# The tail of a four-layer graph network on one core: the last two row pairs, instead of one, taken tile by tile with plain products

## Chip, core and metric

The kernel runs on one NeuronCore of a Trainium2 chip. The time is device microseconds of that core for one launch; lower is better. Engine names are those of the profile: PE is TensorE's matmul, PEld its weight load, DVE is VectorE, ACT is ScalarE, POOL is GpSimd, SP is SyncE, which here issues the DMAs.

## What is computed

Input x has 128 graphs of 64 nodes with 512 features (8192 rows), in float32; adj is one 64 x 64 graph for all of them. Four layers follow each other, each as x = layernorm(x + layer(x)).

```python
# layer 0: sum of messages
deg[:, None] * (x @ Wi.T + b) + adj @ (x @ Wj.T)
# layer 1: four attention heads, an output layer with attention, a feed-forward part
h   = elu(gat(x, adj, W_heads, a_heads))     # 4 heads, 512 -> 512 each
out = elu(gat(h, adj, W_out, a_out))         # 2048 -> 512
y   = relu(out @ w1 + b1) @ w2 + b2 + out
l1  = (y - mean) / sqrt(var + 1e-5) * gamma + beta
# layers 2 and 3: one attention head each
attn = softmax(where(adj, leaky(e_src[i] + e_dst[j], 0.2), -inf))
l2  = attn @ (x @ W)
```

gat is the same kind of attention with a leak of 0.01. The score vectors e_src and e_dst are dot products of rows of x with W @ a.

## The kernel before

**Tiles and pairs.** A tile is 128 rows (two graphs). T = 2 tiles make a pair of 256 rows, and there are NP = 32 pairs, numbered 0 to 31. Aggregation over the neighbours is done first (A x), then the product with the weights. Most products are Strassen-Winograd products of a 2 x 2 split: `strassen` (L685) and `seven` (L633) take seven products of half size instead of eight. For a pair the split is by tile, by halves of the inner dimension and by halves of the 512 output columns, so that each product is a chain of matmuls with 256 columns into the PSUM tiles stx and sty. The seven weight factors (11, 12, 21, 22 and the sums T1 to T4) are computed once on POOL (`stage_stream`, L580), stored in DRAM, and streamed in for every pair by `part_from` (L613): the 512-row weights into a ring called "ws" with NWS = 4 places, the 256-row ones (w2, W2, W3) into "wk" with 6. The sums on the data side are POOL's too (`sums`, L709).

**Stages of a pair.** `stage_first` (L887) is layer 0; `stage_scores` (L937) the heads' scores (f), the attention and the aggregated rows ys; `stage_heads` (L1007) the four heads (PSUM tiles stx_h, sty_h, results hT); `stage_project` (L1044) the product with W_out (stx_o, sty_o, result who) and the dots for the output attention (f_1o). `stage_out` (L1084) is the output attention (`out_attention`, L1068: transposes bc_1o and pt_1o, attention rows e_1o and aT_1o), the aggregation op, elu, the transposes oTp, w1 (hidp), w2 (stx_y, sty_y), and the norms. `stage_gat` (L1138) is layer 2 or 3: dots with the rows r (f), `attention` (L819: bc, e, pt), the copy to aT, the aggregation gp, and the product with W2 or W3 (stx, sty). `stage_late` (L1289) runs `stage_out` and both `stage_gat`.

**The last pair.** Pair 31 ends otherwise. `stage_last` (L1192) loads w2, W2 and W3 as they are (raw, named w2_last, W2_last, W3_last), b2 and gamma (rows_last), does the output attention of the pair and loads the score rows of both layers. `stage_tile` (L1209) then takes each of the two tiles by itself from the aggregation op on: w1 for 128 rows, and w2, W2 and W3 as plain products, `plain` (L1216), four matmuls of 512 columns into yp and z. Its attention is that of one tile (64 columns instead of 128), and `norms` (L855) and `normalize` (L737) are as for the others. `moments` (L726) puts the two steps of 1/sqrt(var) on POOL (rs).

**What sets the order.** The program text doesn't: every call is recorded as a step (`Plan.note`, L188). The stages are generators that a queue of due times advances (`start`, L1303, and the loop behind it, in units of TURN = 107); a step's number in this recording is its rank. `Plan.play` (L327) adds to the rank the value of LATER (L48) for the step's engine and tile name, with S or E for the first 11% and the last 7% of all steps. `Plan.order` (L229) is a list scheduler: with a cost for each call and a hand-over time (WAIT, L41), it gives each engine the ready step of the lowest rank, and gives out the places of the pools. The order that comes out is what is emitted; on the chip each engine takes its steps in that order. All instructions have the line of the call in `play`, 336, so this text tells them apart by tile names.

**The lines around the change**, from the loop that starts the stages (L1314):

```python
at, pace, rest = {NP - 2: (2.0, 0.8, 0.0), NP - 1: (1.3, 0.6, 0.0)}.get(
    p, (1.42, 1.0, 5.0)
)
if p < NP - 1:
    start(TURN * (p + at), 10 * p, stage_late(p, pace, rest))
else:
    start(TURN * (p + at), 10 * p, stage_last(p))
    for t in range(T):
        start(TURN * (p + at), 10 * p + 1 + t, stage_tile(p, t))
```

Of the kernel before, what the change touches and what calls it, by code (L numbers as in the profile page):

```python
# [12 lines left out]
FP = mybir.dt.float32  # L13
# [7 lines left out]
P = 128  # L21
EPS = 1e-5
NEVER = -3.0e38
T = 2
TURN = 107.0
# [2 lines left out]
NA = 2  # L28
NWS = 4
NWK = 6  # L30
UNITS = 3
AHEAD = 4

# [4 lines left out]

WAIT = 0.152  # L41
NEAR = 150
SLACK = {"tensor": 0.8, "sync": 0.4}

# [1 line left out]


LATER = {  # L48
    "gp:never/S": -100, "gp:rs_i": -60, "gp:s_o/S": -20, "gp:ys/E": -40, "sc:aT": -100,
    "sc:aTg/S": 20, "sc:elu/S": -40, "sc:hT": 120, "sc:oT": 60, "sc:who": -80, "sc:xT": -200,  # L50
    "sc:xT/S": -180, "sc:ys/S": 132, "sy:beta/S": -12, "sy:raw_w": 180, "te:fp/S": -20,
    "te:hidp/E": -40, "te:hidp/S": 28, "te:l": 29, "te:l/S": 69, "te:pt": -28, "te:pt/E": 200,
    "ve:e": -29, "ve:e/S": 40, "ve:f_o/S": -120, "ve:hT": 100, "ve:has": 200, "ve:mv": -100,
    "ve:mv/E": 100, "ve:mx": -20, "ve:o": -140, "ve:r": -40, "ve:r/E": 40, "ve:sh": 10,
    "ve:sm": -80, "ve:st": -13,
}


# [315 lines left out]
def gnn_stack_kernel(  # L374
# [24 lines left out]
    nc = Plan(tc)  # L399
    NT, D = x.shape  # L400
    N = adj.shape[0]
    H = W_heads.shape[0]
# [30 lines left out]
    def rows(srcs, name, tag="rows"):  # L433

        bufs = {"rows": 2, "A": NA}.get(tag, 1)
        t = unit.tile([P, 2, D], FP, tag=tag, bufs=bufs, name=f"rows_{name}")
        for i, src in enumerate(srcs):
            nc.sync.dma_start(out=t[:, i, :], in_=src.partition_broadcast(P))
        return t
# [66 lines left out]
    score = {}  # L506
# [561 lines left out]
    def out_attention(p):  # L1068

        while p not in outs:  # L1070
            yield 1.0
        who, f = outs.pop(p)
        pt = yield from attention(
            f, 0.01, mask1, fill1.to_broadcast([P, N]), None, f"1o_{p}"
        )
        aT = unit.tile([P, T, N], FP, tag="aT", bufs=2, name=f"aT_1o_{p}")
        with nc.soon():
            for b in range(2):
                for t in range(T):
                    nc.scalar.copy(aT[ts(b, N), t, :], pt[ts(t, N), ts(b, N)])  # L1080
        yield 2.0
        return who, aT
# [106 lines left out]

    shared = {}  # L1190

    def stage_last(p):  # L1192

        raw = {}
        for name, src, tag, bufs in (("w2", w2, "ax", 1), ("W2", W2, "ys", 2), ("W3", W3, "ys", 2)):
            raw[name] = unit.tile([P, KC, D], FP, tag=tag, bufs=bufs, name=f"{name}_last")
            nc.sync.dma_start(out=raw[name], in_=src.rearrange("(c p) o -> p c o", p=P))
        r = unit.tile([P, 2, D], FP, tag="hT", bufs=H, name="rows_last")
        for i, src in enumerate((b2, gamma)):
            nc.sync.dma_start(out=r[:, i, :], in_=src.partition_broadcast(P))  # L1200
        who, aT = yield from out_attention(p)
        o = xp.tile([P, T, D], FP, tag="x", name=f"o_{p}")
        shared.update(raw=raw, rows=r, who=who, aT=aT, o=o)
        yield 2.0
        for name in ("2", "3"):
            shared[name] = rows([score[name][s, :] for s in range(2)], f"{name}_{p}")
            yield 2.0

    def stage_tile(p, t):  # L1209

        while "3" not in shared:
            yield 1.0
        x, o, r, raw = xs[p][:, t, :], shared["o"][:, t, :], shared["rows"], shared["raw"]
        who, aT = shared["who"], shared["aT"]

        def plain(lhsT, w, into, name):  # L1216
            ps = psum.tile([P, D], FP, tag="b", name=name)
            for k in range(KC):
                nc.tensor.matmul(
                    ps, lhsT=lhsT(k), rhs=w[:, k, :], start=(k == 0), stop=(k == KC - 1)  # L1220
                )
            nc.vector.tensor_tensor(into, ps, into, ALU.add)

        ps = psum.tile([P, D], FP, tag="b", name=f"op_{p}_{t}")
        with nc.together():
            for b in range(2):
                nc.tensor.matmul(
                    ps[ts(b, N), :], lhsT=aT[ts(t, N), b, :], rhs=who[ts(t, N), b, :],
                    start=True, stop=True,
                )  # L1230
        elu(o, ps)
        yield 3.0
        both = unit.tile([P, 2, KC, P], FP, tag="A", bufs=NA, name=f"oT_{p}_{t}")
        oT, hid = both[:, 0, :, :], both[:, 1, :, :]
        ps = psum.tile([P, KC, P], FP, tag="b", name=f"oTp_{p}_{t}")
        with nc.together():
            for k in range(KC):
                nc.tensor.transpose(ps[:, k, :], o[:, ts(k, P)], ident)
        nc.scalar.copy(oT, ps)
        nc.gpsimd.tensor_tensor(o, o, r[:, 0, :], ALU.add)  # L1240
        yield 3.0
        ps = psum.tile([P, KC, P], FP, tag="b", name=f"hidp_{p}_{t}")
        for c in range(KC):
            with nc.together():
                for k in range(KC):
                    nc.tensor.matmul(
                        ps[:, c, :], lhsT=w1_sb[:, k, ts(c, P)], rhs=oT[:, k, :],
                        start=(k == 0), stop=(k == KC - 1),
                    )
        for c in range(KC):  # L1250
            nc.scalar.activation(
                hid[:, c, :], ps[:, c, :], AF.Relu, bias=b1_sb[:, c : c + 1]
            )
        yield 4.0
        plain(lambda k: hid[:, k, :], raw["w2"], o, f"yp_{p}_{t}")
        norms(o, x, r[:, 1, :], f"{p}_{t}")
        yield 8.0
        for name in ("2", "3"):
            f = small.tile([P, 2], FP, tag="f1", name=f"f_{name}_{p}_{t}")
            for s in range(2):  # L1260
                junk = unit.tile([P, D], BF, tag="junk", name=f"j_{name}_{p}_{t}_{s}")
                nc.vector.tensor_tensor_reduce(
                    junk, x, shared[name][:, s, :], 1.0, 0.0, ALU.mult, ALU.add,
                    accum_out=f[:, s : s + 1],
                )
            yield 2.0
            pt = yield from attention(
                f.unsqueeze(2), 0.2, mask2, never.to_broadcast([P, N]), has, f"{name}_{p}_{t}", 1
            )
            aT = unit.tile([P, P], FP, tag="s3", bufs=2, name=f"aT_{name}_{p}_{t}")  # L1270
            nc.gpsimd.memset(aT, 0.0)
            for b in range(2):
                nc.scalar.copy(aT[ts(b, N), ts(b, N)], pt[:, ts(b, N)])
            yield 2.0
            gT = unit.tile([P, KC, P], FP, tag="s2", bufs=2, name=f"gT{name}_{p}_{t}")
            ps = psum.tile([P, KC, P], FP, tag="b", name=f"gp{name}_{p}_{t}")
            with nc.together():
                for c in range(KC):
                    nc.tensor.matmul(
                        ps[:, c, :], lhsT=x[:, ts(c, P)], rhs=aT, start=True, stop=True  # L1280
                    )
            nc.scalar.copy(gT, ps)
            yield 3.0
            plain(lambda k: gT[:, k, :], raw[f"W{name}"], x, f"z{name}_{p}_{t}")
            normalize(x, f"{name}_{p}_{t}")
            yield 6.0
        nc.sync.dma_start(out=out[ts(p * T + t, P), :], in_=x)

    def stage_late(p, pace, rest):  # L1289

        for later in stage_out(p):
            yield later * pace
        for name in ("2", "3"):
            yield rest
            for later in stage_gat(p, name):
                yield later * pace
# [6 lines left out]
    def start(at, order, stage):  # L1303
        heapq.heappush(queue, (at, order, stage))

    for p in range(NP):
        if p < AHEAD:
            start(TURN * (0.2 * p - 1.2), 10 * p + 4, stage_first(p))
        else:
            start(TURN * (p - 1.1), 10 * p + 4, stage_first(p))  # L1310
        start(TURN * (p - 0.5), 10 * p + 3, stage_scores(p))
        start(TURN * (p + 0.6), 10 * p + 2, stage_project(p))

        at, pace, rest = {NP - 2: (2.0, 0.8, 0.0), NP - 1: (1.3, 0.6, 0.0)}.get(  # L1314
            p, (1.42, 1.0, 5.0)
        )
        if p < NP - 1:
            start(TURN * (p + at), 10 * p, stage_late(p, pace, rest))
        else:
            start(TURN * (p + at), 10 * p, stage_last(p))  # L1320
            for t in range(T):
                start(TURN * (p + at), 10 * p + 1 + t, stage_tile(p, t))
    start(0.0, 10 * NP, stage_heads())
    start(-1.15 * TURN, 0, score_weights(
        [head_rows(w) for w in w_h], a_h, "h", lambda h: head_sums(w_h[h])
# [67 lines left out]
```

## Time and profile before

| | |
|---|---|
| median of 3 runs | 3310.98 us (3309.94 to 3311.04) |
| the profiled execution | 3313.95 us, span 3312.2 us |
| PE busy | 3265.2 us, 21268 matmul records |
| PE weight load busy | 2881.8 us |
| DVE, ACT, POOL busy | 2374.4, 1364.6, 1724.0 us |
| DMA | 726.08 MB, mean 219 GB/s |
| granted PE clock | 0.994 |

The span reaches from the first to the last instruction of the core. A float32 matmul appears as two records. In a row of a group, the name left of the arrow is the tile written, then the tiles read, then the shape. A wait row reads "who waited <- for whom: total, times, longest". Names have lost their numbers: stx_o is the PSUM tile of any pair's W_out product, z that of any plain product with W2 or W3. PE's matmuls are pipelined, so that the length of a record is more than the distance to the next one; distances between starts are used here where a price is needed.

### The profile page before, as it was taken

The numbers are of one execution on the slowest core, as the hardware profiler recorded it, in microseconds if no ns is written. First come the engines' busy times: TensorE is split into PE (matmuls) and PEld (weight loads), VectorE is DVE, ScalarE is ACT, GpSimd is POOL, SyncE is SP. The second block draws the span as 40 slices with busy tenths as digits, with TensorE's granted clock in tenths as the row PEclk, the third lists the DMA queues.
The fourth block names the chain that finished last, engine by engine and source line by source line (L and its number), as shares of the span: only waits on it lengthen the run. The fifth ranks groups of instructions, "written<-read, shape, count | busy, mean of one in ns | idle before, by whom it ended". The sixth has DMA issues, their size and how long they took to land.

```text
span 3312.2 us, 60000 instructions
## 1 busy us (share of the span) xinstructions
PE 3265.2 (99%) x21268; PEld 2881.8 (87%) x21268; DVE 2374.4 (72%) x5668; ACT 1364.6 (41%) x3226; POOL 1724.0 (52%) x1860
## 2 busy tenths in 40 slices
PE   8999999999999999999999999999999999999997
PEld 4888888898988989989889988888889899898885
DVE  5467767777777777777777777777777767777766
ACT  2434344343444434444443443434444344343442
POOL 6745445554555555455454555645554455554442
PEclk9999999999999999999999999999999999999998
DMA  8956666767667676667766667676666766667652
GB/s 303 338 177 215 221 203 215 234 208 237 211 210 233 213 247 197 200 230 221 242 204 220 212 217 236 214 226 208 214 233 208 246 201 202 229 216 238 227 183 77
DMA packets 306584, 726.08 MB, mean 219 GB/s; under 512 B 34240, under 2 KB 43504, under 8 KB 306288
## 3 DMA queue, kind: packets, MB, share of 16 engines
q1 hardware_dynamic: 306288, 722.26, 67.1%
q8 instruction: 171, 2.80, 0.3%
q14 instruction: 125, 1.02, 0.1%
HBM read 688.69 MB, written 33.44 MB: 218 GB/s over the span
## 4 chain that ended last, share of the span: by engine, by line
PE 91%; DVE 4%; DMA 3%; POOL 1%; issue 1%; ACT 0%; SPq 0%; POOLq 0%; DVEq 0%; ACTq 0%
PE stx_h L336 13%; PE stx_o L336 13%; PE stx L336 12%; PE sty_h L336 10%; PE sty_o L336 9%; PE sty L336 9%; PE hidp L336 7%; PE yp L336 4%; PE gp L336 3%; PE stx_y L336 3%; PE sty_y L336 2%; PE axp L336 2%; PE l L336 1%; PE op L336 1%; PE oTp L336 1%; DMA d_f<-f 1%
## 5 line engine op out<-in xcount | busy, mean ns | idle before, releaser
L336 DVE CUSTOM_DVE_ANT_0 j<-x,rows 128x512 bf16<-128x512 f32 x736 | 584.1, 794 | 94.3 <-DMA rows<-d_h 75.6
L336 PE MATMUL stx_h<-ys,wh 128*128 128x128 f32 x3072 | 403.8, 275 | 0.7 <-DVE hT L336 0.7
L336 PEld LDWEIGHTS stx_h<-ys,wh 128*128 128x128 f32 x3072 | 381.1, 192 | 22.3 <-DVE sh L336 5.7
L336 POOL TENSOR_SCALAR rs<-mv 128x1 f32<-128x1 f32 x256 | 104.1, 407 | 406.2 <-DVE mv L336 392.2
L336 ACT COPY hT<-stx_h 128x256 f32<-128x256 f32 x384 | 143.0, 372 | 384.6 <-PE stx_h L336 378.6
L336 ACT ACTIVATE x<-x,sh,rs 128x512 f32<-128x512 f32 x256 | 207.2, 813 | 223.6 <-DVE sh L336 221.0
L336 PE MATMUL sty_h<-ys,wh 128*128 128x128 f32 x2048 | 273.8, 277 | 0.0
L336 PEld LDWEIGHTS sty_h<-ys,wh 128*128 128x128 f32 x2048 | 254.4, 192 | 9.0 <-issue 0.5
L336 PE MATMUL stx_o<-ws_wo_T,s_o 128*128 128x256 f32 x1024 | 246.0, 383 | 0.5 <-ACT who L336 0.5
L336 DVE TENSOR_TENSOR x<-stx,x 128x256 f32<-128x256 f32 x360 | 150.8, 420 | 132.1 <-PE stx L336 131.0
L336 PE MATMUL sty_o<-ws_wo,hT 128*128 128x256 f32 x1024 | 243.2, 380 | 0.1
L336 PE MATMUL hidp<-oT,w 128*128 128x256 f32 (+1 forms) x1056 | 228.9, 373 | 0.0
L336 PEld LDWEIGHTS hidp<-oT,w 128*128 128x128 f32 x1056 | 194.0, 190 | 24.9 <-ACT oT L336 0.2
L336 PEld LDWEIGHTS stx_o<-ws_wo_T,s_o 128*128 128x128 f32 x1024 | 190.2, 191 | 28.4 <-ACT who L336 2.1
L336 PEld LDWEIGHTS sty_o<-ws_wo,hT 128*128 128x128 f32 x1024 | 190.8, 191 | 25.6 <-issue 1.1
L336 DVE SCALAR_TENSOR_TENSOR hT<-elu,hT 128x512 f32<-128x512 f32 x256 | 174.9, 684 | 43.3 <-ACT elu L336 41.3
L336 POOL TENSOR_TENSOR ys<-ys,t 128x256 f32<-128x256 f32 x128 | 102.9, 814 | 189.8 <-PE sty_h L336 189.4
L336 ACT ACTIVATE elu<-hT 128x512 f32<-128x512 f32 x256 | 153.0, 599 | 108.7 <-DVE hT L336 104.6
L336 POOL TENSOR_TENSOR rs<-rs,mhalf 128x1 f32<-128x1 f32 x256 | 173.4, 677 | 21.1
L336 DVE BATCH_NORM_STATS2 st<-x 128x6 f32<-128x512 f32 x256 | 176.5, 689 | 5.1
L336 DVE TENSOR_TENSOR hT<-sty_h,hT 128x256 f32<-128x256 f32 x256 | 107.2, 420 | 81.2 <-PE sty_h L336 69.3
L336 ACT COPY ys<-yp 128x512 f32<-128x512 f32 x256 | 132.2, 602 | 78.4 <-PE yp L336 71.7
(205 smaller groups left out, 7629.3 us busy)
## 6 DMA issues: line engine op xcount, KB each, us to landing
ws_wo_T<-d_wo_T SPq DMA_DIRECT2D x256, 512.0 KB, 3.9
ws_wo<-d_wo SPq DMA_DIRECT2D x192, 512.0 KB, 5.3
ws_W_T<-d_W_T SPq DMA_DIRECT2D x248, 256.0 KB, 4.2
rows<-d_h SPq DMA_DIRECT2D x240, 256.0 KB, 4.7
ws_w_T<-d_w_T SPq DMA_DIRECT2D x112, 512.0 KB, 4.9
ws_W<-d_W SPq DMA_DIRECT2D x186, 256.0 KB, 4.1
ws_w<-d_w SPq DMA_DIRECT2D x84, 512.0 KB, 5.2
rows<-d SPq DMA_DIRECT2D x128, 256.0 KB, 4.3
```

What stands on the lines that cost most here:

```text
L336: getattr(getattr(self.tc.nc, s.engine), name)(*map(real, args), **{k: real(v) for k, v in kw.items()})
```

## The change

Pair 30 now ends as pair 31 did: its output attention is done for the pair, and from the aggregation op on each of its tiles runs through `stage_tile`, with hidp for 128 rows at a time and plain products with w2, W2 and W3. `stage_last` is split. What all four tiles share (the raw weights, b2, gamma, and the score rows) is loaded by `stage_last()` once; the score rows of layer 2 now stand in a place of the "hT" pool and those of layer 3 in one of the "ws" ring. `stage_out_last(p)` does the output attention of one pair; o of pair 30 is in the "o" pool, that of pair 31 in the "x" pool as before. LAST holds the due times of these stages. WAIT goes from 0.152 to 0.153, and the LATER values are another list (36 entries before, 50 now).

```diff
+LAST = (2.0, 1.3, 1.0)
...
-WAIT = 0.152
+WAIT = 0.153
...
 LATER = {
-    "gp:never/S": -100, "gp:rs_i": -60, "gp:s_o/S": -20, "gp:ys/E": -40, "sc:aT": -100,
...
+    "gp:bones": -160, "gp:fill": -140, "gp:hT/S": -20, "gp:never/S": -100, "gp:o": 200,
+    "gp:raw_W": 40, "gp:raw_W/S": -80, "gp:raw_wo/S": -100, "gp:rs/E": 180, "gp:rs_i": -400,
...
+    "sc:who": -80, "sc:xT/S": -320, "sy:d_w_T/S": 26, "sy:degb": 31, "sy:degb/S": 13,
+    "sy:raw_wo": 40, "sy:ws_wo_T": -280, "te:fp/S": -20, "te:hidp/S": 28, "te:l": 20,
...
-    def stage_last(p):
+    def stage_last():
...
-        who, aT = yield from out_attention(p)
-        o = xp.tile([P, T, D], FP, tag="x", name=f"o_{p}")
-        shared.update(raw=raw, rows=r, who=who, aT=aT, o=o)
+        shared.update(raw=raw, rows=r)
         yield 2.0
         for name in ("2", "3"):
-            shared[name] = rows([score[name][s, :] for s in range(2)], f"{name}_{p}")
+            tag, bufs = {"2": ("hT", H), "3": ("ws", NWS)}[name]
+            shared[name] = unit.tile([P, 2, D], FP, tag=tag, bufs=bufs, name=f"rows_{name}_last")
+            for s in range(2):
+                nc.sync.dma_start(
+                    out=shared[name][:, s, :], in_=score[name][s, :].partition_broadcast(P)
+                )
             yield 2.0
 
+    def stage_out_last(p):
+
+        who, aT = yield from out_attention(p)
+        if p == NP - 1:
+            o = xp.tile([P, T, D], FP, tag="x", name=f"o_{p}")
+        else:
+            o = unit.tile([P, T, D], FP, tag="o", name=f"o_{p}")
+        shared[p] = who, aT, o
+        yield 0.0
+
     def stage_tile(p, t):
 
-        while "3" not in shared:
+        while "3" not in shared or p not in shared:
             yield 1.0
-        x, o, r, raw = xs[p][:, t, :], shared["o"][:, t, :], shared["rows"], shared["raw"]
-        who, aT = shared["who"], shared["aT"]
+        x, r, raw = xs[p][:, t, :], shared["rows"], shared["raw"]
+        who, aT, o = shared[p]
+        o = o[:, t, :]
...
-        if p < NP - 1:
-            start(TURN * (p + at), 10 * p, stage_late(p, pace, rest))
+        if p < NP - 2:
+            start(TURN * (p + 1.42), 10 * p, stage_late(p, 1.0, 5.0))
         else:
-            start(TURN * (p + at), 10 * p, stage_last(p))
+            at = TURN * {NP - 2: NP - 2 + LAST[0], NP - 1: NP - 1 + LAST[1]}[p]
+            start(at, 10 * p, stage_out_last(p))
             for t in range(T):
-                start(TURN * (p + at), 10 * p + 1 + t, stage_tile(p, t))
+                start(at, 10 * p + 1 + t, stage_tile(p, t))
+    start(TURN * (NP - 1 + LAST[2]), 10 * NP - 1, stage_last())
```

More of the change, by code (lines that the diff above doesn't have):

```diff
@@ L48 @@
 LATER = {
-    "gp:never/S": -100, "gp:rs_i": -60, "gp:s_o/S": -20, "gp:ys/E": -40, "sc:aT": -100,
[L50 to L55, printed above, removed]
+    "gp:bones": -160, "gp:fill": -140, "gp:hT/S": -20, "gp:never/S": -100, "gp:o": 200,
+    "gp:raw_W": 40, "gp:raw_W/S": -80, "gp:raw_wo/S": -100, "gp:rs/E": 180, "gp:rs_i": -400,
+    "gp:s_o": -20, "gp:wh/S": 40, "gp:ys/E": -60, "sc:aT": -120, "sc:bc": -80, "sc:sm": -140,
+    "sc:who": -80, "sc:xT/S": -320, "sy:d_w_T/S": 26, "sy:degb": 31, "sy:degb/S": 13,
+    "sy:raw_wo": 40, "sy:ws_wo_T": -280, "te:fp/S": -20, "te:hidp/S": 28, "te:l": 20,
+    "te:l/S": 100, "te:pt": 4, "te:pt/E": 200, "te:stx_o/E": 40, "ve:bc/S": -120, "ve:e": -64,
+    "ve:e/S": 40, "ve:e_o/E": -40, "ve:f/E": 40, "ve:f_o": -24, "ve:f_o/S": -120, "ve:hT": 140,
+    "ve:has": 220, "ve:mv": -160, "ve:mv_i/E": 40, "ve:ng": 140, "ve:ng/S": 80,
+    "ve:nm_o/S": 120, "ve:r": -60, "ve:sh": 10, "ve:sm": -100, "ve:st": -13, "ve:x": 80,
+    "ve:x/E": -80,
 }
@@ L1312, in gnn_stack_kernel @@
         start(TURN * (p + 0.6), 10 * p + 2, stage_project(p))
-        at, pace, rest = {NP - 2: (2.0, 0.8, 0.0), NP - 1: (1.3, 0.6, 0.0)}.get(
-            p, (1.42, 1.0, 5.0)
-        )
-        if p < NP - 1:
-            start(TURN * (p + at), 10 * p, stage_late(p, pace, rest))
-        else:
-            start(TURN * (p + at), 10 * p, stage_last(p))
+        if p < NP - 2:
+            start(TURN * (p + 1.42), 10 * p, stage_late(p, 1.0, 5.0))
+        else:
+            at = TURN * {NP - 2: NP - 2 + LAST[0], NP - 1: NP - 1 + LAST[1]}[p]
+            start(at, 10 * p, stage_out_last(p))
             for t in range(T):
-                start(TURN * (p + at), 10 * p + 1 + t, stage_tile(p, t))
+                start(at, 10 * p + 1 + t, stage_tile(p, t))
+    start(TURN * (NP - 1 + LAST[2]), 10 * NP - 1, stage_last())
     start(0.0, 10 * NP, stage_heads())
```

## Prediction

> **What bounds the kernel now.** I read the page's totals first, then busy time by stage, then who TensorE (PE) waits for, then its records in the tail.
>
> ```profile
> PE 3265.2 (99%) x21268; PEld 2881.8 (87%) x21268; DVE 2374.4 (72%) x5668; ACT 1364.6 (41%) x3226; POOL 1724.0 (52%) x1860
> ```
>
> PE is the bound; 47 us of 3312.2 are its idle time. The stages say where (columns: length; busy and count of PE, weight loads, DVE, ACT, POOL; granted clock; DMA share; GB/s):
>
> ```profile
> 0.00:200.00 200.00, 185.68 (x1094) 138.13 (x1095) 110.31 (x258) 74.04 (x160) 131.04 (x119) 0.97 0.85 295
> 200.00:3204.00 3004.00, 2994.22 (x19798) 2681.50 (x19797) 2195.12 (x5216) 1256.98 (x2975) 1560.07 (x1685) 1.00 0.68 219
> 3204.00:3232.00 28.00, 24.98 (x131) 20.54 (x130) 17.29 (x43) 9.77 (x29) 12.38 (x17) 1.00 0.48 149
> 3232.00:3256.00 24.00, 20.84 (x112) 15.30 (x111) 20.66 (x53) 8.72 (x24) 8.96 (x17) 0.95 0.28 85
> 3256.00:3284.00 28.00, 19.23 (x60) 11.51 (x58) 17.82 (x62) 7.38 (x19) 6.29 (x13) 0.80 0.27 80
> 3284.00:3312.20 28.20, 20.21 (x80) 14.80 (x80) 13.15 (x42) 7.70 (x20) 5.29 (x11) 0.80 0.13 47
> ```
>
> 3004 us in the middle lose 10 us. The last 108 us lose 23, and their clock falls to 0.80. DVE is as busy as PE from 3232 to 3284. PE's waits from 3190 on, and in the first 200 us (total, times, longest):
>
> ```profile
> PE bc L336 <- DVE f L336: 6.0, 3, 3.5
> PE sty L336 <- ACT gT L336: 2.4, 1, 2.4
> PE gp L336 <- ACT aTg L336: 2.2, 3, 0.8
> ```
>
> ```profile
> PE x1Tp L336 <- ACT ax L336: 2.0, 1, 2.0
> ...
> PE sty_h L336 <- POOL t L336: 1.5, 1, 1.5
> PE stx_o L336 <- DMA ws_wo<-d_wo: 1.1, 1, 1.1
> ```
>
> So the tail is a chain through DVE (f: the score sums of layers 2 and 3) that PE can't fill. PE's records in the tail (start, length):
>
> ```profile
> 3205.78 7.07 PE L336 MATMUL hidp<-oT,w 128*128 128x256 f32 x32
> ...
> 3232.83 7.39 PE L336 MATMUL hidp<-oT,w 128*128 128x128 f32 x64
> ...
> 3242.28 5.32 PE L336 MATMUL yp<-w_last,oT 128*128 128x512 f32 x12
> ...
> 3264.87 2.08 PE L336 MATMUL z<-W_last,gT 128*128 128x512 f32 x2
> ...
> 3272.92 4.46 PE L336 MATMUL z<-W_last,gT 128*128 128x512 f32 x10
> 3283.16 0.48 PE L336 MATMUL bc<-ident,f 128*128 128x128 f32 x1 [3.49 <-DVE f L336]
> ```
>
> A matmul is two records. A 128x512 record costs 0.43 us (12 fill 5.2) at full clock, and 1.03 in the pair at 3264.87, after a pause.
>
> **The Trainium skill.** "TensorE: Matmul & The Clock Gate", Part 1, says that PE falls to half clock after an idle window of about 3.4 us and needs a busy one to come back. The trace agrees: after 3277-3284, nearly idle, records take double until 3291. The same page's head table calls VectorE's queue a strict FIFO; so do I treat DVE below. "SBUF: State Buffer", "Who interferes with whom", says that a DVE operation with two SBUF inputs shuts out a GpSimd one that reads SBUF: the rstd step on POOL takes 0.22 us alone and 0.78 beside the gamma product.
>
> **The change, part by part.** The order of the changed program, set against the old one engine by engine, shows three stretches: the start (PE's first 280 of 4450 rows) partly changed, the middle the same but for some swaps, the last 5% changed.
>
> *Products.* For pair 30, w2, W2 and W3 go from 28 records of 128x256 (8 take 1.73 us, so 6.05) to 16 of 128x512 (6.9): +0.85 three times. hidp goes from 7.07 to 7.39. Together +2.9 us of PE. Strassen's sums on POOL (ten of 0.73 us) go; they lay beside PE. DVE comes out even: a product's adds fall from 2.8 us (five of 0.42, one of 0.69) to two of 0.69, but the attention of a layer, done for each tile at 64 columns, takes 2x1.76 instead of 2.2. The DMAs of 21 factors (256 KB each) and of pair 30's own rows go too; the queue was at 0.48 and less of its share there, so I count nothing.
>
> *The last W_out product.* I take as zero the start of its seventh factor for pair 31 (stx_o, T4), 3204.05 before. In the new order hidp of pair 30 (7.2), one tile's w2 product (3.45) and a transpose (0.1) stand before it, which came after it before. What feeds hidp is covered: between op of pair 30 and its transposes lie two W_out factors (3.5 us; elu of a tile takes 0.6+0.6+0.7). So PE stays busy and zero comes **10.8** later.
>
> *From zero to the end: 108.15 us before.* I walked the new rows by hand, each at its duration in the tail's groups and 0.15 to 0.2 us per handover.
> - To the end of op for pair 31: before 16.3. After: DVE first has, in program order between the add of yp and the last step of pair 31's output attention, 6 dots and 5 BN statistics (0.72 apart), 7 wide two-input operations (0.69-0.76), 5 of 256 columns (0.42), and small ones: 4.3+3.6+5.1+2.1+3.1 = 18.2 us. PE has only 12.4 us there. The transpose comes at 19.4, op ends at **21.7**. Before, hidp lay over these dots; now it is spent ahead of them. PE waits 7 us at pt_1o; queued behind it are op of pair 31, pair 30's first gp and W2 product and the last W3 factor of pair 29, none of which can pass.
> - To the end of yp of tile 31_0: before 23.6, after **19.3**: hidp can begin 26.8 after zero (elu of two tiles behind ACT's other work, transposes), and from there PE is full with hidp 7.2, the tile's w2 product 3.5 and, between them, a W2 product of pair 30, 3.45: 40.95 after zero.
> - To the end of tile 31_0's W2 product: before 29.8, after **26.1**. The step from yp to the next scores' transpose stays 12.3 (12.2 before: norms, two rstd, dots); only pair 30's W2 and W3 products fill it, and PE waits 3.3, 2.7 and 1.2.
> - To the end of 31_1's W3 product: before 30.4, after **23.3**, since pair 30 has left the queue; waits of 2.4 and 2.7.
> - To the end: before 8.0, after **6.9** (add, statistics, rstd, activation, 3.0 to land).
>
> Sum 97.3. Waits of 7, 3.3, 3.9, 2.4 and 3.4 us will drop the clock again. Before, the same cost 7.9 us, which is in the 108.15. I take 1.4+0.5+3.5+0.8+2.6 = 8.8 for now (5 to 12). So 106.1, and 10.8+106.1-108.15 = **+8.75**.
>
> *Weight ring.* rows_3_last holds one of four "ws" places while W_out's factors are streamed; a factor then has 5.3 us of PE work to land in, and 512 KB took 5.9 (median) in that stretch, 3.9 over the run. I take +0.75 (0 to 3). SP's queue is in order: the three raw weights (1 MB each, issued earlier now) wait for the heads' buffers with factors behind them; 11 us of PE work lie between the last head and the first of these factors, against 1.5 MB at some 300 GB/s (5 us); without that cover the factor would be late by what is over.
>
> *Start.* The new LATER values, WAIT and three LAST numbers are no instructions: they act through the order alone. degb's load moves behind the first heads' weights, so x+degb starts near 24.6 us rather than 10.8; POOL was idle 12 us from 20 to 50, which hides it, or 2 us are lost if not. Then W_out's sums on POOL (2.35 us each) all come before the heads' t1, so its factors are stored sooner, and by POOL's new row pair 1's t1 comes at about 122 rather than 126.8. That takes the waits of 1.5 and 1.1 and perhaps part of the 2.0. But from 181 us DVE makes PE wait in an order that hasn't changed, so some returns. I take **-2.5** (-4.5 to +1).
>
> Sum +8.75+0.75-2.5 = +7.0. Against the profiled execution (span 3312.2, 1.75 around it, 3313.95) that is 3321; against the median 3310.98, **3318**.
>
> **Rivals.**
> 1. *The clock stays up* (not slower). If PE's short transposes keep the windows from counting as idle, the 8.8 becomes about 3, and the start gives its whole 4.5 with no ring loss: 3310.98+8.75-5.8-4.5 = 3309.5. For it: before, pauses of 0.8 and 1.7 us cost no clock. Against: the stretches with 2.4+0.7 us and more all did. It decides at a pause of about 2 us: if the waits at pt_1o and behind it stay below that, which takes DVE's 18.2 us down to 14, slower is off.
> 2. *The ring starves* (slower still). Five factors late by 1 us each in place of my 0.75, and 1.75 for the clock: 3318+6 = 3324. For: 5.9 against 5.3. Against: the same factors came in time before.
> 3. *The staggering pays* (faster). If the chains run shorter than my rows say, because no Strassen adds (0.42-0.69 each) stand between the steps of a norm any more: stage one by 4, stages three and four by 2 each, and with that 5 less of half clock and the whole 4.5 at the start: 3310.98+8.75-4-4-5-4.5 = 3302. For: stages three to five already lose 12 us together. Against: the walk took the new rows as they stand.
> That the split does not happen is excluded: the order shows z2_30 and z3_30.
>
> **How the numbers follow.** Forecast +7, in 3313 to 3323: 0.46. Rival 1: 0.25, rival 2: 0.17, rival 3: 0.12. 0.2% is 6.6 us, about what a measurement tells from no change. A quarter of the forecast's cases lie below that: slower 0.34+0.17 = 0.51, same 0.25+0.12 = 0.37, faster 0.12. From 3306 to 3326 leaves out most of rival 3 and the end of rival 2.
>
> **What would show it.** Work: 16 more z records for each of pair 30's W2 and W3, and PE busy up about 3 us at full clock. Zero: T4 of pair 31 after yp of 30_0. Stage one: pt_1o waiting for DVE e_1o, 2.5 us or more. Ring: a wait of stx_o or sty_o for a ws_wo load near 3195. Start: no wait of sty_h for POOL near 126. I am wrong if pair 31's op ends within 14 us of T4's start, or if the clock in the last 100 us is over 0.95.

## The result, and the profile after

| | before | after |
|---|---|---|
| median, 12 runs each on one chip | 3310.64 us (3304.11 to 3316.41) | 3317.27 us (3313.2 to 3323.59) |
| ratio, 95% interval | | 1.002 (1.0012 to 1.0027) |
| median on a second chip, 50 and 13 runs | 3308.68 us | 3316.7 us, ratio 1.0023 (1.0015 to 1.0031) |
| the profiled execution, its span | 3313.95, 3312.2 us | 3318.04, 3316.2 us |

The change makes the kernel 6.6 us (0.2%) slower, 8.0 on the second chip. First the totals of the changed kernel's page, then its stages, cut where the stages of before were cut, by events and not by times (columns as before):

```profile
PE 3265.3 (98%) x21266; PEld 2871.6 (87%) x21266; DVE 2364.0 (71%) x5670; ACT 1363.7 (41%) x3230; POOL 1714.1 (52%) x1854
```

```profile
0.00:200.00 200.00, 183.80 (x1100) 137.94 (x1101) 113.40 (x263) 73.88 (x161) 130.88 (x119) 0.98 0.85 298
200.00:3214.00 3014.00, 3003.15 (x19859) 2687.16 (x19858) 2186.29 (x5216) 1259.07 (x2988) 1558.10 (x1686) 1.00 0.68 218
3214.00:3242.00 28.00, 22.01 (x88) 14.83 (x87) 23.13 (x63) 9.25 (x26) 9.66 (x16) 0.82 0.06 19
3242.00:3266.00 24.00, 23.51 (x124) 15.96 (x124) 13.66 (x38) 7.98 (x24) 7.43 (x15) 1.00 0.03 12
3266.00:3290.00 24.00, 17.68 (x57) 8.54 (x55) 16.60 (x56) 7.03 (x19) 3.90 (x11) 0.93 0.03 12
3290.00:3316.20 26.20, 15.21 (x44) 7.17 (x44) 10.91 (x37) 6.47 (x15) 4.09 (x9) 0.89 0.08 30
```

PE's total is what it was (3265.2 before), so the totals show nothing. The stages do: the first one of the tail, from T4 of pair 31 (the start of the seventh factor of its W_out product) to that pair's op, now has DVE busier (23.1 us of 28) than PE (22.0), at a clock of 0.82; the next is full of PE work. PE's waits from 3190 us on say the same (who waited, for whom, total, times, longest):

```profile
PE bc L340 <- DVE f L340: 7.9, 4, 3.5
PE gp L340 <- ACT aT L340: 3.3, 5, 1.1
PE pt L340 <- DVE e L340: 2.4, 1, 2.4
PE pt_1o L340 <- DVE e_1o L340: 2.1, 1, 2.1
```

In the first 200 us the 1.5 for POOL and 1.1 for a factor's load have become

```profile
PE stx_o L340 <- DMA ws_wo<-d_wo: 2.2, 1, 2.2
...
PE sty_h L340 <- POOL t L340: 1.2, 1, 1.2
PE sty_o L340 <- DMA ws_wo<-d_wo: 1.1, 1, 1.1
```

and PE's records in the tail are (start, length, what; in brackets the idle time before it and its releaser):

```profile
3205.24 7.31 PE L340 MATMUL hidp<-oT,w 128*128 128x128 f32 x64
...
3215.93 1.89 PE L340 MATMUL stx_o<-ws_wo_T,hT 128*128 128x256 f32 x8
...
3231.96 0.47 PE L340 MATMUL bc<-ident,f 128*128 128x128 f32 x1 [3.52 <-DVE f L340]
3234.56 0.45 PE L340 MATMUL pt_1o<-ident,e_1o 128*128 128x128 f32 x1 [2.13 <-DVE e_1o L340]
3235.31 2.65 PE L340 MATMUL op<-who,aT_1o 64*64 64x512 f32 x8 [0.30 <-ACT aT_1o L340]
...
3255.42 5.32 PE L340 MATMUL yp<-w_last,oT 128*128 128x512 f32 x12
```

T4 (stx_o at 3215.93) stands behind hidp and one w2 product of pair 30, as the order said, and op of pair 31 comes 16 us later than before (3219.34).

**A yardstick with less scatter.** One profile of each kernel misleads, since runs of one kernel lie over 10 us apart. The last factor of pair 31's layer 0 (the last record sty<-ws_w,ax, called M here) is the same row of PE's order in all kernels below, and what follows is a fixed program. M came anywhere from 3052.8 to 3060.3 us. From M to the end of the span, two profiles of each kernel agree within 0.2 us. (e8 below, which has the change's order from M on, was 0.8 shorter, with 2.6 us less half clock; so the scatter of one profile is up to 0.8 us.) Before (two profiles), then after (two):

```profile
3059.40:3312.20 252.80, 229.87 (x1336) 193.39 (x1334) 168.66 (x434) 97.23 (x246) 102.53 (x131) 0.95 0.49 162
```

```profile
3052.75:3305.40 252.65, 229.76 (x1336) 193.44 (x1334) 169.96 (x434) 97.22 (x246) 101.79 (x131) 0.95 0.50 162
```

```profile
3058.46:3316.20 257.74, 232.66 (x1334) 185.27 (x1332) 164.05 (x436) 97.12 (x250) 93.46 (x125) 0.96 0.39 131
```

```profile
3057.51:3315.30 257.79, 232.34 (x1334) 184.90 (x1332) 164.59 (x438) 97.69 (x251) 94.42 (x126) 0.96 0.39 131
```

So 5.0 of the 6.6 to 8.0 us lie behind M (4.2 to 5.1 with e8 counted in), well outside that scatter. The rest lies within the scatter of M's arrival and isn't located. In the table "half clock" is the PE time lost to it: busy time times (1 - clock), summed over slices of 1 us. "Work" is what is left of busy time; "idle" includes the 7 us after PE's last matmul. In e7 and e12 "work" includes the added idle transposes (6.8 us of records in e7). The first column is the difference of medians to before, run beside it. Every row is one profile; only before and after have a second.

| kernel | median to before | M to end | idle | half clock | work |
|---|---|---|---|---|---|
| before | (0.7 for itself) | 252.8 | 22.9 | 8.0 | 221.9 |
| after | 6.6, 8.0 | 257.7 | 25.1 | 7.0 | 225.6 |
| e1 code alone | 14.9 | 267.7 | 30.7 | 10.8 | 226.2 |
| e2 places alone | 12.6 | 262.5 | 30.3 | 7.8 | 224.4 |
| e3 T4 early | 14.6 | 266.0 | 27.7 | 10.2 | 228.1 |
| e4 rows in another place | 9.7 | 257.4 | 25.1 | 7.1 | 225.1 |
| e5 less work | 5.4 | 258.0 | 26.6 | 8.0 | 223.4 |
| e6 attention early | 14.9 | 265.7 | 29.2 | 8.8 | 227.7 |
| e7 clock kept up | 2.9 | 254.9 | 20.6 | 1.5 | 232.8 |
| e8 start of before | 8.0 | 257.0 | 26.9 | 4.4 | 225.7 |
| e11 less work, twice | 5.3 | 256.9 | 26.1 | 10.1 | 220.6 |
| e12 before, clock kept up | -1.9 | 249.9 | 17.7 | 3.1 | 229.0 |

### The profile page after: what moved, and what is told of

Read it like the earlier page. It is cut to its first block, busy times and chain, and to the rows that moved or that the text cites. A ratio compares the mean times of both kernels' runs of the same rounds, so it can differ in the third digit from the quotient of the medians.

```text
span 3316.2 us, 59904 instructions
## 1 busy us (share of the span) xinstructions
PE 3265.3 (98%) x21266; PEld 2871.6 (87%) x21266; DVE 2364.0 (71%) x5670; ACT 1363.7 (41%) x3230; POOL 1714.1 (52%) x1854
## 4 chain that ended last, share of the span: by engine, by line
PE 59%; DVE 2%; DMA 1%; POOL 0%; issue 0%; ACT 0%; SPq 0%; POOLq 0%; DVEq 0%
PE stx_h L340 9%; PE stx_o L340 8%; PE stx L340 8%; PE sty_h L340 7%; PE sty_o L340 6%; PE sty L340 6%; PE hidp L340 4%; PE yp L340 3%; PE gp L340 2%; PE stx_y L340 2%; PE sty_y L340 1%; PE axp L340 1%; PE z L340 1%; DMA ws_w<-d_w 1%; PE op L340 1%; PE oTp L340 1%
## 5 line engine op out<-in xcount | busy, mean ns | idle before, releaser
L340 DVE CUSTOM_DVE_ANT_0 j<-x,rows 128x512 bf16<-128x512 f32 x720 | 569.4, 791 | 95.8 <-DMA rows<-d_h 74.9
L340 PEld LDWEIGHTS sty_o<-ws_wo,hT 128*128 128x128 f32 x1024 | 191.0, 191 | 26.9 <-DMA ws_wo<-d_wo 1.3
L340 ACT COPY ax<-axp 128x512 f32<-128x512 f32 x128 | 68.4, 589 | 242.5 <-PE axp L340 235.7
```

The lines of the kernel that those rows point to most:

```text
L340: getattr(getattr(self.tc.nc, s.engine), name)(*map(real, args), **{k: real(v) for k, v in kw.items()})
```

## Experiments

The theory at the start: T4's place behind hidp is what costs, with the plain products second. The rivals: the products' own work, half clock, the weight ring, the start.

### 1. Is it the code, the places, T4, or the ring?

e1 is the changed code with the old LATER and WAIT; e2 the old code with the new ones. e3 and e4 are one-line edits of the changed kernel:

```diff
# e3
-    "te:stx_o/E": 40
+    "te:stx_o/E": -60
# e4
-            tag, bufs = {"2": ("hT", H), "3": ("ws", NWS)}[name]
+            tag, bufs = {"2": ("hT", H), "3": ("hT", H)}[name]
```

> The changed code (two pairs tile by tile, plain products) with the old table of order: pair 31's last W_out factor, T4, stands ahead of pair 30's hidp again, and the start is the old one. Order theory (T4 behind hidp_30 and yp_30_0 is what costs): some 9 us of PE work of pair 30 fill the 7 us for which PE waits for VectorE between T4 and op_31, the start gives its 1.2 us back, so about 3311.5 us, 3309 to 3314, on the side of before. Rival 'the plain products' own 2.9 us of PE work and their half clock cost': 3316 to 3319, as the change. Rival 'the wait for the ring places': 3316 to 3319.

> The old code (pair 30 still in Strassen products, one pair tile by tile) with the new table of order: the new start, and T4 behind hidp_30. Order theory: before, plus the 7 to 9 us by which T4 is late, less 1.2 at the start and nothing for plain products: 3315 to 3320 us. Rival 'the plain products cost': the new start's gain alone remains, 3308 to 3311. Rival 'ring': the place that the third layer's rows hold is not taken here, 3308 to 3311 too.

> The changed kernel with one entry of its table changed: the end products of W_out's stx_o fall due 60 earlier instead of 40 later, which puts T4 of pair 31 ahead of hidp_30; start, ring and plain products stay as in the change. Order theory: PE's 7 us of waiting between T4 and op_31 are filled, so 3308 to 3312 us, 5 to 9 below the change. Every rival (half clock in the tail, ring, the plain products' work): 3316 to 3319, no gain.

> The changed kernel with the rows of the third layer in a place of hT instead of one of the ring of four weight places, so that the ring keeps four for its products to the end. Order theory: the 1.1 us of waits for W_out's handover go at most, 3316 to 3317.5 us. Rival 'the ring starves': 3309 to 3313.

Measured: e1 3323.07 us (ratio to before 1.0044, 1.0032 to 1.0057), e2 3320.77 (1.0033, 1.002 to 1.0045), e3 3322.79 (1.0045, 1.0031 to 1.0059), e4 3317.93 (1.0027, 1.0019 to 1.0036).

e1 and e3 lie above every range that was expected. e3 does what it should: T4 starts 147.9 us after M and not 157.5. But op of pair 31 comes 180.6 us after M where it came 176.9 after, and the end is 8 us later. DVE's records in e3 show why (start, length):

```profile
3211.84 0.69 DVE L340 CUSTOM_DVE_ANT_0 j_1o<-who,rows_1o 128x512 bf16<-128x512 f32 x1
3212.45 0.08 DVE L340 DVE_READ_ACCUMULATOR2_ANT f_1o<- 128x1 f32 x1
...
3223.74 0.58 DVE L340 TENSOR_TENSOR e_1o<-bc_1o,f_1o 64x128 f32<-64x128 f32 x2
...
3232.49 0.29 DVE L340 TENSOR_TENSOR e_1o<-e_1o,r_1o 128x128 f32<-128x128 f32 x1
```

and PE's, the transpose between the two:

```profile
3222.52 0.38 PE L340 MATMUL bc_1o<-ident,f_1o 128*128 128x128 f32 x2
```

The dots are done 158.6 us after M, 7.1 sooner than in the change, but bc_1o stands in PE's queue behind pair 30's w2 products and comes 10 us after them (1.3 us after them in the change). Then pair 30's norms stand between the steps of e_1o on DVE, 9.0 us from the first to the last, much as in the change (8.5). So T4's place alone does not set op's time in the new code: with T4 early, op waits for bc_1o and e_1o in its place.

e1 and e2 are slower than both kernels that they are made from: the old places cost the new code 10.0 us behind M, the new places the old code 9.7. A list of places goes with its code. The plain products can't be judged by e1, nor the places by e2, since 50 entries change at once. Still, e2 came close to what the order theory expected of it (3315 to 3320), and its trace has T4 8.1 us later after M than before, op 9.3 later and the end 9.7 later (M is at 3056.49 here):

```profile
3209.27 1.89 PE L339 MATMUL stx_o<-ws_wo_T,hT 128*128 128x256 f32 x8
...
3225.76 1.07 PE L339 MATMUL op<-who,aT_1o 64*64 64x512 f32 x4
```

So for the old code the theory is neither shown nor refuted. e4, in which a few rows of the order trade places too, shows that the row place in the ring is not at fault: the wait for a ws_wo load before hidp stays at 0.8 us (0.5 and 0.9 in the two profiles after). Nor does the new list bring such waits by itself: e2 has none before hidp, while e1, the new code with the old list, has 1.9 us of waits for W_out's factors there.

### 2. The products' work, op's place, the clock, the start

e5 leaves out the last quarter of the sum in three plain products of pair 30, so that these outputs lack it (the steps stay in the plan without a call, so that nothing else moves); e6 adds to e3; e7 puts idle transposes into pauses; e8 uses before's LATER for the first ninth of the steps.

```diff
# e5, in plain
+            last = KC - 2 if (p, t) == (NP - 2, 1) else KC - 1
...
-                    ps, lhsT=lhsT(k), rhs=w[:, k, :], start=(k == 0), stop=(k == KC - 1)
+                    ps, lhsT=lhsT(k), rhs=w[:, k, :], start=(k == 0), stop=(k == last)
                 )
+                if k > last:
+                    nc.steps[-1].calls = []
# e6, in play, on top of e3
+                if any(re.fullmatch(r"(bc|e|nm|sm|r|pt|aT|f|j)_1o_31\w*", str(t.args.get("name"))) for t in s.uses):
+                    s.rank -= 300
# e7, in play
+WARM = {"bc_2_30_0": 16, "pt_1o_31": 12, "bc_2_31_0": 16, "pt_3_31_1": 12}
...
+                    for _ in range(WARM[warm[0].args["name"]]):
+                        self.tc.nc.tensor.transpose(real(where), real(ident)[:, : where.shape[0]], real(ident))
```

> The changed kernel with one of the eight chunk products left out of each plain product of pair 30 (w2, W2 and W3: the last quarter of the sum for its second tile), so that pair 30 has the PE work that it had in Strassen factors; the outputs of those tiles lack that part. The order of everything else is that of the change, instruction for instruction. 6 matmuls of 0.43 us go, 2.6 us. Work theory (PE's extra work counts in full, wherever it lies): 2.6 us below the change, 3314 to 3316. Rival 'the tail waits for VectorE, so that PE's work there is hidden': no gain, 3316 to 3319.

> The kernel with T4 early, and beside it every step of pair 31's output attention (bc_1o, e_1o, pt_1o and what lies between) 300 places earlier in what falls due, so that VectorE no longer puts steps of pair 30 between those of e_1o: pt_1o and op_31 stand ahead of pair 30's bc on PE. Theory 'op_31 starts the last pair's walk, and its time sets the end' (T4 was only one thing ahead of it): op_31 some 5 us earlier and the end 4 to 6 below the kernel with T4 early, 3316 to 3319. Rival 'the end is set by PE's work and by the pauses in the tail, however the two walks are laid': op_31 earlier, but the pauses come later instead, 3320 to 3325.

> The changed kernel with idle transposes of a constant (16, 12, 16 and 12 of them, 1.3 to 1.9 us each group) put on PE into the four pauses of 2.1 to 3.5 us of its tail, into the PSUM place that the waiting transpose takes next; nothing else moves. In the profile of the change three stretches of half clock begin in these pauses and cost 7 us of PE time. Clock theory: they go, and half or more of it comes off the end, 3311 to 3315. Rival 'PE waits for VectorE right after, so that a slow PE costs nothing': 3316 to 3319; if the idle transposes themselves run late, 3318 to 3321.

> The changed kernel with the table of order of before for the first ninth of the steps: PE's order is that of before for its first 570 instructions and that of the change from 630 on. In the profiles the new start was 1.1 us ahead at 230 us. Theory 'the start is worth what it shows': 0.5 to 1.5 us above the change, 3317.5 to 3319. Rival 'the new start loses in the first 300 us what the waits for W_out's first factors cost': 1 to 3 below, 3314 to 3316.

Measured: e5 3314.25 us (1.0019, 1.0011 to 1.0026), e6 3323.84 (1.0044, 1.0031 to 1.0057), e7 3311.83 (1.0012, 1.0004 to 1.002), e8 3316.86 (1.0023, 1.0014 to 1.0032).

e6: op comes 5.0 us sooner after M than in e3 (175.6), as expected, and the end only 0.3 sooner. The pauses come later instead: bc waits 6.0 us for f, in place of 1.9. First e3's line from hidp to the end, then e6's:

```profile
PE bc L340 <- DVE f L340: 1.9, 2, 1.4
```

```profile
PE bc L342 <- DVE f L342: 6.0, 5, 2.5
```

So in these orders an earlier op of pair 31 doesn't bring an earlier end, and the result lies in the rival's range. But op is only 1.3 us sooner than in the change here; no run of the new code brought it near the 159.9 us after M of before.

e8: the start is worth nothing that these runs can tell. Its interval, 4.6 to 10.6 us above before, covers that of the change run again (e9 below), and is too wide to exclude a gain or a loss of 2 us. Its profile was 2.2 us ahead of the change's at 230 us and 1.9 behind at M, though PE's order is the change's from its 630th instruction on.

e7 lies in the range of the clock theory. PE's records around the first two filled pauses (compare with the lines of after above; line 344 is the added transposes):

```profile
3223.27 1.91 PE L344 MATMUL bc<-ident 128*128 128x128 f32 x16
3226.95 0.32 PE L346 MATMUL bc<-ident,f 128*128 128x128 f32 x1 [1.77 <-DVE f L346]
3227.11 1.47 PE L344 MATMUL pt_1o<-ident 128*128 128x128 f32 x12
3229.55 0.30 PE L346 MATMUL pt_1o<-ident,e_1o 128*128 128x128 f32 x1 [0.97 <-DVE e_1o L346]
3230.15 1.76 PE L346 MATMUL op<-who,aT_1o 64*64 64x512 f32 x8 [0.29 <-ACT aT_1o L346]
```

The eight records of op take 1.76 us, not 2.65, and a bc 0.32, not 0.47. The bc itself comes as before the edit, 4.55 us after the start of the factor ahead of it; that is DVE's doing. But half clock no longer follows any of the four filled pauses; the one stretch that is left (3271.75 to 3275.5) comes after three unfilled ones. Behind M the half clock falls from 7.0 to 1.5 us, and the stretch from 257.7 to 254.9. Against before, the medians fall from 6.6 or 8.0 to 2.9, though the intervals of the two ratios overlap.

e5's median is 5.4 us above before, 1.3 less than the change's first median and 2.6 less than its second, so it fits the work theory and a smaller gain alike, and its profile shows no gain behind M (258.0). That asked for a larger dose.

### 3. Controls, a double dose, and the other kernel

e9 and e10 are the two kernels themselves. e11 leaves a chunk out for both tiles of pair 30 (p == NP - 2 in e5's first line). e12 is before with idle transposes:

```diff
+WARM = {
+    "sty_2_30": 14, "bc_2_31_1": 6, "pt_2_31_0": 4, "pt_2_31_1": 8, "bc_3_31_0": 20, "pt_3_30": 3,
+}
```

> The changed kernel once more, as the measure for the other runs of this set, and for a second profile of it. Every theory: 6.6 us above before, within 4 to 9. In its profile the time from pair 30's hidp to the end should be 107 to 112 us (111.0 in the first), whatever the start and the middle took.

> The kernel before once more, beside itself: 0 us, within 1.5, and a second profile of it. The time from pair 30's hidp to the end was 106.4 us in the first, with 8 us of PE time lost to half clock. Work theory: that stretch is the shorter one by T4 (1.7) and the plain products (2.6) in every profile, 104 to 107. Rival 'the first profile of before had more half clock than most of its runs': 101 to 104, and then pauses and clock are part of what the change costs.

> The changed kernel with a chunk product left out of each plain product of both tiles of pair 30 (the last quarter of the sum in w2, W2 and W3, so that these outputs lack it), in unchanged order: 12 matmuls of 0.43 us, 5.2 us. Work theory (PE's work in the tail counts in full): 5.2 us below the change, 4 to 6. Rival 'VectorE sets the pace there': 0 to 2.5 below.

> The kernel before with idle transposes of a constant (14, 6, 4, 8, 20 and 3) in six pauses of its tail, 0.6 to 3.5 us long, at which three stretches of half clock begin; nothing else moves. Clock theory (as the 8 us of loss in its profile): 3 to 5 us below before, 3304 to 3306, and faster than both kernels. Rival: VectorE and the idle transposes take it back, 0 to 1 below.

Measured: e9 3316.7 us (1.0023, 1.0015 to 1.0031), e10 3309.37 (1.0003, 0.9994 to 1.0012), e11 3313.99 (1.0019, 1.0012 to 1.0025), e12 3306.74 (0.9992, 0.9984 to 0.9999).

e10 speaks against the rival that the first profile of before was an odd one: from hidp of pair 30 to the end it took 106.3 us, 106.4 in the first, and half clock took 7.8 us behind M, 8.0 in the first. After takes 111.0 and 111.2.

e11 answers e5: 5.2 us of matmuls less give 2.7 us in the medians, just above the range of the rival (0 to 2.5) and below that of the work theory (4 to 6), and 0.9 behind M, which is hardly more than the scatter there. The line from M on, and PE's waits from 3205 us on:

```profile
3055.83:3312.70 256.87, 230.76 (x1322) 185.02 (x1320) 163.90 (x436) 97.10 (x250) 93.57 (x125) 0.95 0.39 132
```

```profile
PE bc L340 <- DVE f L340: 8.8, 4, 3.6
PE pt L340 <- DVE e L340: 2.7, 1, 2.7
PE pt_1o L340 <- DVE e_1o L340: 2.1, 1, 2.1
PE pt L340 <- DVE nm L340: 1.8, 1, 1.8
```

The 12 records are gone (1334 to 1322) and the work falls by 5.0 us, but idle grows by 1.0 and half clock by 3.1 (10.1 us, where the three profiles with the change's own work and order behind M, those of after, e9 and e8, have 4.4 to 7.0). So little of PE's work counts in full here. The reading that fits is that PE and the chain of norms and softmax through DVE, POOL and ACT are about equally long: what PE saves comes back as waiting and, more so, as half clock.

e12 is faster than both kernels, by 0.08% against before. The interval ends just below 1, and the gain is less than the 3 to 5 us expected. Behind M it is 2.9 us:

```profile
3055.93:3305.80 249.87, 232.12 (x1391) 196.19 (x1389) 168.72 (x434) 97.13 (x246) 101.99 (x131) 0.98 0.50 164
```

One stretch of half clock is left in it while PE works, from 3278 to 3285, after pauses of 1.7 and 1.3 us with the 20 transposes between them. With idle transposes in both, the kernel before is still the shorter one by 5.0 us (249.9 against 254.9), with 3.1 and 1.5 us of half clock left. So half clock doesn't make the difference between the two kernels.

## Why the prediction was right, and where its steps were not

3318 was forecast and 3317.27 measured, 0.7 us off. The shape of the sum holds: T4 comes late, and what follows it gets shorter by less. But that it came so close is luck. The terms behind M were forecast at +9.5 together (8.75 and 0.75) and measured +5.0. Ahead of M -2.5 was forecast, and the medians leave +1.6 to +3.0 there, which the scatter doesn't let one locate. The two errors cancelled.

- **T4 later, +10.8, and the ring, +0.75.** Measured from M, T4 starts 144.7 us after it before and 157.5 after: +12.8, where the two terms give 11.55. The order was read rightly: M to hidp takes 146.4 before, T4's 1.7 us among them, and 146.8 after, without T4. So 2.1 us are lost there that before didn't lose. PE had no wait in that stretch before; after it has three, 1.2 us in all:

```profile
PE stx_o L340 <- DMA ws_wo<-d_wo: 0.5, 1, 0.5
PE sty_o L340 <- DVE who L340: 0.5, 1, 0.5
PE sty_y L340 <- DMA ws_w<-d_w: 0.2, 1, 0.2
```

  The other 0.9 are matmuls that follow each other a little less closely; what does that stays open. The ring's term had the right size (0.5 and 0.9 us of waits for ws_wo) and the wrong cause: with the rows elsewhere (e4) the load still comes late, so it is not the missing place. Such waits come with the new code under the old list too (e1) and not with the new list on the old code (e2). The raw weights, which the prediction named beside the ring and which are issued earlier now, are one candidate that no run tests.
- **From zero to the end, 106.1 instead of 108.15.** Measured 100.3 and 100.5. Stage by stage, forecast (full clock) and measured: 21.7 and 22.0; 19.3 and 19.2; 26.1 and 27.5; 23.3 and 24.8; 6.9 and 6.9. The walk by hand was good in sum: its 97.3 without half clock is 97.1 in e7, where little is left.
- **Half clock, +8.8.** This is the mis-sized term: 3 us (100.3 less 97.1, or less 97.3). The pauses were forecast at their right places, most of them too long (pt_1o and bc together 5.7 for 7; then 2.6, 0.9 and 1.2 for 3.3, 2.7 and 1.2; then 1.4 and 2.4 for 2.4 and 2.7). The stretches that began in them covered op, some transposes, a W3 factor and part of an aggregation (the first) and most of a plain product (each of the others). PE loses 7 us of busy time to them (8 before), and the path takes less than half of that; that PE waits for DVE there anyway is the likely reason, not a shown one. To that extent rival 1 was right; its other part, that the clock stays up, was not: it was 0.91 over the last 102 us.
- **Start, -2.5.** No gain shows, and e8 can't exclude one of that size. The wait for POOL near 126 us moved to 94 us and became 1.2, and new ones of 1.1 and 2.2 us for W_out's first factors came, at 121 and 126 us. So what POOL gave, the loads may have taken back.
- **Products, +2.9 us.** The records came as said: 64 of z for 32, and work behind M is up by 3.7 us. The sum had this in the walk, not as a term of its own, and rightly so: e11 shows that this work is worth about half its length at the end by the medians, and less than a fifth by the stretch from M.

Of the signs named, all but one came: 3.7 us more work (behind M, not in PE's total), T4 after yp of 30_0, the wait for ws_wo before 3195, no wait for POOL near 126, op's end 22.0 us after T4's start. The wait at pt_1o was 2.1 (2.3 in e9) and not 2.5 us or more; a bc that waits 3.5 for f stands ahead of it.

What isn't borne out is the reading behind the sum, that T4's place costs and pair 31's op carries the cost on. In the new code, moving T4 ahead (e3), or the attention steps with it (e6), leaves the end 8 us later, not sooner. What the change costs behind M, 5.0 us, is by the table 3.7 of work and 2.2 more idle, less 1.0 of half clock; on the side of time it is 0.4 us more to hidp though T4 is not yet done, and 4.7 from hidp to the end, of which 1.7 is T4. That says where the 5.0 us stand, not what causes them: no run took them back from the change while leaving before as it is.

Not settled: what causes the 5.0 us; whether an op of pair 31 as early as before would help the new code; whether the plain products alone would cost less in an order found for other places of the same code, since every other order tried here was worse; what the 1.6 to 3.0 us are by which medians differ more than the stretch from M; and e11 with the clock kept up, which wasn't tried and would tell how much of its lost gain is the clock's.

## What to carry to other kernels

Where a scheduler's list goes with one version of the code, undoing half of a change tells little: each half alone was 5 to 10 us worse than the whole, measured behind M. Compare the stretch behind an instruction that all versions share, not whole spans; two profiles of a kernel agreed within 0.2 us there (0.8 with e8), where the spans of the two profiles of before differ by 6.8. In a tail in which PE waits for the vector chain again and again, count neither extra work nor an earlier instruction in full, and try idle matmuls in the pauses first: they took 3 us off the stretch behind M in both kernels without moving anything (1.9 us in the medians of before).

## What the runs showed of the hardware

The stretches of half clock are 3.5, 7 or 10 us long (after: 3232 to 3242, 3269.5 to 3273, 3300 to 3303.5; e9: 3231.5 to 3238.5 and 3296.5 to 3303.5), which agrees with the free-running window of about 3.4 us that the Trainium skill gives in "TensorE: Matmul & The Clock Gate", Part 1. The page speaks of an idle window. Here pauses of 2.6 and 2.4 us, shorter than that window, went ahead of the second and the third stretch (3.5 us without a matmul ahead of the first), so a window need not be idle throughout. Nor does a pause's length decide alone, as the 2 us at which the prediction let rival 1 turn would have it. In the second profile of the same kernel (e9) the same 2.6 us were not followed by half clock; it came 8.7 us later, after pauses of 2.2, 0.7 and 0.4 us. The same rows, first in after, then in e9:

```profile
3269.58 0.48 PE L340 MATMUL bc<-ident,f 128*128 128x128 f32 x1 [2.63 <-DVE f L340]
3269.85 4.22 PE L340 MATMUL z<-W_last,gT 128*128 128x512 f32 x6
```

```profile
3267.30 0.32 PE L340 MATMUL bc<-ident,f 128*128 128x128 f32 x1 [2.63 <-DVE f L340]
3267.46 2.74 PE L340 MATMUL z<-W_last,gT 128*128 128x512 f32 x6
...
3276.15 2.08 PE L340 MATMUL z<-W_last,gT 128*128 128x512 f32 x2
```

In after, e9 and e8, half clock began in or right after one of the first two pauses that e7 fills (bc, pt_1o), and again at the last (pt). With 1.5 to 1.9 us of transposes of a constant in each it came at none of them (e7, one profile), so such transposes can keep the clock up. With 5.2 us of PE work left out the half clock was 10.1 us and not 7.0 (e11, one profile): less work can go with a slower clock for what is left.
